# Attention's row sums and turned outputs on VectorE and by transfers within SBUF, beside the products with the values

## The chip, the cores and the metric

The kernel runs on one core of a Trainium2 chip. The metric is the device time of one execution in microseconds (us); before the change it is 2896.16 us, the median of three runs (2895.83 to 2897.63). Engines: TensorE (PE, and PEld for its weight loads), VectorE (DVE), ScalarE (ACT), GpSimd (POOL) and SyncE (SP), which here only issues transfers.

## What is computed

32 batches of a 512 x 512 matrix go through two graph layers that share one adjacency matrix. The first is attention with 8 heads of 64, masked by the adjacency matrix, then a residual and a layer norm without weights; the second multiplies by the adjacency matrix and a weight, again with a residual and a layer norm. Everything is float32.

```python
q, k, v = ((x @ W + b).reshape(b, n, 8, 64) for ...)
scores = einsum('bihd,bjhd->bhij', q, k) / sqrt(64) + where(adj == 0, -1e9, 0)
out = einsum('bhij,bjhd->bihd', softmax(scores), v)
x = layernorm(x + out)                     # layer 0
x = layernorm(x + (adj @ x) @ weight + bias)   # layer 1
```

## The kernel before

All 32 batches are unrolled into one program without loops on the chip; the order of every engine's instructions is written out by hand (a manual schedule), and each engine executes its own in that order. A wait holds everything behind it on its engine. `b` is the batch, `g` one of its two groups of four heads, `hp` one of its four pairs of heads (two in a group), `j` or `c` one of four blocks of 128 rows.

Scores are kept transposed: keys in the partitions, queries along the row. `scores` makes a group's scores pair by pair and block by block: two products with 64 rows of the array each (L555) into two PSUM banks, VectorE adds the mask and writes the tile `e` (L557), ScalarE takes the exponential in place (L559). GpSimd adds the four blocks of a pair into `es` (L570, `add_exponentials`), 128 x 1024 for two heads. `attend` multiplies by the values (L579) into one bank, a head's output in 64 partitions, so that the output too is transposed, and ScalarE copies it to `attT` (L582).

A row sum of the softmax is the sum of `es` over the partitions. `add_up` takes it on TensorE, by a product with ones (L590) for each head into 32 partitions of one bank; ScalarE copies it to `total` and adds it up for a check of the range (L596). `invert` turns `total` with four transposes on TensorE (L603), and VectorE takes the reciprocal (L605). `residual` turns `attT` with four transposes on TensorE for each pair (L612); VectorE multiplies by the reciprocals (L615) and adds to the rows of `x` (L617). After the last pair of a batch it calls `statistics` (L421, L422) for the layer norm, four blocks, each over whole rows.

All PSUM tiles come from `bank`, eight banks in turn. The main loop goes over (b, g): the products with the values of the group's pairs, `add_up`, the scores of the next group, then other work (`units_of`) by `work_until`, with `invert` and `residual` at set shares of it. That other work is: in the first half of a batch the projections of q and k of the next batch (L359, seven block products by Strassen's scheme each, evicted by VectorE and ScalarE), in the second half the rest of v, the product with the adjacency matrix of the batch before (`aggregate`, L478) and its convolution with the weight (`convolve`, seven block products, also L359). `convolve` evicts with VectorE: L531 adds a bank to `x`, for blocks 6 and 7 L527 updates the tile `mix` from the bank and GpSimd adds `mix` to `x` (L529); blocks run in the order 1, 2, 5, 6, 7, 3, 4, and the additions of 3 and 4 go to rows that GpSimd has added to. `flips` turns the input of the batch after next: VectorE's 32 x 32 transposes (L343, `turn_squares`), and GpSimd's four sums for Strassen's factors (`sum_rows`, L349, L321 to L323). VectorE's transpose turns each 32 x 32 square in its place only; that is why the input of those batches is loaded in squares of 32 columns (`load_squares`, L246: 16 transfers of 512 pieces of 128 B), which puts the squares in the places where they belong. The same sums for the aggregated rows are at the end of `aggregate` (L321 to L323).

SP issues in one queue: `load_squares(b + 2)`, which waits for the tiles `xin`, then in `turn_over` the store of batch b - 2 (L462) and the load of `x` of batch b (L231) into the same tile, which waits for the store to land. After the last group there is a tail for the last two batches.

Of the kernel before, what the change touches and what calls it, by code (L numbers as in the profile page):

```python
# [32 lines left out]
FP = mybir.dt.float32  # L36
# [3 lines left out]
AF = mybir.ActivationFunctionType  # L40
# [5 lines left out]
P = 128  # L46
# [159 lines left out]
def fast_kernel(ctx: ExitStack, tc, verdict, x, adj, Wq, bq, Wk, bk, Wv, bv, W1, b1, out):  # L206
# [14 lines left out]
    def bank(*shape):  # L221

        return psum.tile([P, *shape], FP, name="bank", tag="bank", bufs=8)
# [47 lines left out]

    ident = consts.tile([P, P], FP, name="ident")
    make_identity(nc, ident)
    ones = consts.tile([P, P // GROUP], FP, name="ones")
    nc.gpsimd.memset(ones, 1.0)
    eps = consts.tile([P, 1], FP, name="eps")
    nc.gpsimd.memset(eps, EPS)

    sums = consts.tile([P, B * (H // GROUP)], FP, name="sums")
    inverses = consts.tile([P, NB, GROUP], FP, name="inverses")  # L280
    nc.gpsimd.memset(inverses, 0.0)


# [54 lines left out]
    def turn_squares(b, d):  # L338

        if d == 0:  # L340
            XT[b] = work.tile([P, 7, 2, half], FP, name="yT" if b == 1 else "xT", bufs=1)
        xt = XT[b]
        nc.vector.transpose(xt[:, d // 2:d // 2 + 3:2, d % 2, :],  # L343
                            IN[b, d].rearrange("p j f -> p (j f)").rearrange("p (a n) -> p a n", a=2))
# [51 lines left out]
    def flips(b):  # L396

        return [(turn_squares if b else x_transpose, b, c) for c in range(NB)] + [(sum_rows, b)] if b < B else []
# [140 lines left out]
        return [(convolve, b, i) for i in (1, 2, 5, 6, 7, 3, 4)] if b >= 0 else []  # L539


    E, ES, AT, TOTAL, INVERSE = {}, {}, {}, {}, {}
    PAIRS = GROUP // 2

    def scores(b, g):
# [26 lines left out]
    def attend(b, hp):  # L572
        po = bank(N)
        for j in range(NB):
            e = E.pop((b, hp, j))
            for s in range(2):
                h = 2 * (hp % 2) + s
                values = V[b][hp // 2][:, j, h * HD:(h + 1) * HD]
                nc.tensor.matmul(po[s * HD:(s + 1) * HD, :], values, e[:, s, :],  # L579
                                 start=(j == 0), stop=(j == NB - 1))  # L580
        AT[b, hp] = work.tile([P, N], FP, name="attT")
        nc.scalar.activation(AT[b, hp], po, AF.Copy)  # L582

    def add_up(b, g):

        width = P // GROUP
        pm = bank(N)
        for h in range(GROUP):
            es = ES[b, (g * GROUP + h) // 2][:, h % 2, :]
            nc.tensor.matmul(pm[h * width:(h + 1) * width, :], ones, es, start=True, stop=True,  # L590
                             tile_position=(0, h * width))
        for hp in range(g * PAIRS, (g + 1) * PAIRS):
            ES.pop((b, hp))
        total = TOTAL[b, g] = work.tile([P, N], FP, name="total", bufs=1)
        at = b * (H // GROUP) + g
        nc.scalar.activation(total, pm, AF.Copy, accum_out=sums[:, at:at + 1])  # L596

    def invert(b, g):

        total = TOTAL.pop((b, g))  # L600
        pt = bank(NB, GROUP, P // GROUP)
        for c in range(NB):
            nc.tensor.transpose(pt[:, c, :, :], total[:, c * P:(c + 1) * P], ident)  # L603
        inverse = INVERSE[b, g] = work.tile([P, NB, GROUP], FP, name="inverse")
        nc.vector.reciprocal(inverse, pt[:, :, :, 0])  # L605
        nc.gpsimd.tensor_add(inverses, inverses, inverse)

    def residual(b, hp):
        at = AT.pop((b, hp))
        pt = bank(NB, 2, HD)  # L610
        for c in range(NB):
            nc.tensor.transpose(pt[:, c, :, :], at[:, c * P:(c + 1) * P], ident)  # L612
        first = 2 * hp % GROUP
        inverse = INVERSE[b, 2 * hp // GROUP][:, :, first:first + 2]
        nc.vector.tensor_mul(pt, pt, inverse[:, :, :, None].to_broadcast([P, NB, 2, HD]))  # L615
        cols = X[b][:, :, hp * P:(hp + 1) * P]
        nc.vector.tensor_add(cols, pt.rearrange("p c s d -> p c (s d)"), cols)  # L617
        if hp == HP - 1 and b < B - 1:
            for c in range(NB):
                statistics(b, 0, c)  # L620


    def judge():
        seen = consts.tile([P, 3], FP, name="seen")
        nc.vector.tensor_reduce(seen[:, 0:1], sums, axis=AX.X, op=ALU.add)
        nc.vector.tensor_reduce(seen[:, 1:2], inverses, axis=AX.XY, op=ALU.add)
        nc.vector.tensor_reduce(seen[:, 2:3], inexact, axis=AX.X, op=ALU.add)
        well = consts.tile([P, 3], FP, name="well")
        nc.vector.tensor_scalar(well[:, 0:2], seen[:, 0:2], BOUND, None, op0=ALU.is_le)
        nc.vector.tensor_scalar(well[:, 2:3], seen[:, 2:3], 0.0, None, op0=ALU.is_equal)  # L630
        nc.vector.tensor_mul(well[:, 0:1], well[:, 0:1], well[:, 1:2])
        nc.vector.tensor_mul(well[:, 0:1], well[:, 0:1], well[:, 2:3])
        return well[:, 0:1]


    def run(units):
        for unit in units:
            unit[0](*unit[1:])
# [10 lines left out]
        run(first[9 + c:10 + c])  # L649
    run(first[13:16])  # L650
    later = scores(0, 0)
    run(first[16:18] + later + first[18:] + [(look_for_low_half, c) for c in range(NB)] + flips(1))

    def norm(t, which):

        if t - which < 0:
            return []
        lo, hi = which * NB, (which + 1) * NB
        return [(square_root, t, slice(lo, hi)), (invert_root, t, slice(lo, hi))] + [
            (normalise, t, slot) for slot in range(lo, hi)]  # L660
# [5 lines left out]
    def weighed(units):  # L666

        weight = {project: 0.5, aggregate: 0.55, x_transpose: 0.13, convolve: 0.5}
        return [(u, weight.get(u[0], 0.0)) for u in units]

    def units_of(b):

        made, turned = projections(b + 1), flips(b + 2)
        splits, gathered = aggregation(b - 1)
        young, old, seen = norm(b - 1, 0) if b < B - 1 else [], norm(b - 1, 1), survey(b - 2)
        ready = [(turn_over, b)] if 1 < b < B - 1 else []
        if b == B - 1:


            older = convolution(b - 2)  # L680
            lows = [(split_low, b - 1, d) for d in range(DB - 1)]
            units = weighed(lows[:2] + older[:3] + lows[2:] + splits[3:] + older[3:] + gathered + seen)
            return units, [sum(w for _, w in units)] * 2

        if old:
            both = [[(f, b - 1, slice(0, 2 * NB))] for f in (square_root, invert_root)]
            behind = [seen[:2], seen[2:]] + both + [old[2:4], old[4:] + ready] + [[u] for u in young[2:]]
        else:
            behind = [ready] + [[u] for u in young]
        if b == 0:  # L690
            behind = [[]] + [[(sum_weights, w1, n)] for n in range(4)]
        behind += [[] for _ in range(11 - len(behind))] + [splits[:1], [], splits[1:2]]
        units = []
        for k, unit in enumerate(made[:16]):
            units += [unit] + (behind[k] if k < len(behind) else [])
        first = sum(w for _, w in weighed(units))
        values = made[16:]
        units += values[:3] + gathered[:1] + splits[2:3] + gathered[1:2] + values[3:] + splits[3:]
        if b == B - 2 > 0:
            units += [(load, B - 1)]  # L700
        units += gathered[2:3] + turned[:1] + gathered[3:]
        convolved = convolution(b - 1) if b < B - 2 else []
        for k in range(7):
            units += convolved[k:k + 1] + turned[k + 1:k + 2]
        units = weighed(units)
        return units, [first, sum(w for _, w in units)]

# [2 lines left out]
    for i, (b, g) in enumerate(groups):  # L710
# [19 lines left out]

        for hp in range(g * PAIRS, (g + 1) * PAIRS):
            attend(b, hp)
        add_up(b, g)
        if i == len(groups) - 1:
            break
        later = scores(*groups[i + 1])
        if g == 0 and b + 2 < B:
            load_squares(b + 2)
        work_until(0.35)
        invert(b, g)  # L740
        work_until((0.6 if b != B - 2 else 1.0) if g else 0.85)
        for hp in range(g * PAIRS, (g + 1) * PAIRS):
            residual(b, hp)
# [5 lines left out]
        release()  # L749
    t = B - 1  # L750
    rest, last = convolution(t - 1), convolution(t)
    run(rest[:1])
    invert(t, GROUPS - 1)
    for hp in range(HP - PAIRS, HP):
        residual(t, hp)
    old, seen = norm(t - 1, 1), survey(t - 1)
    run(old[:1] + rest[1:2] + old[1:])
    if t > 1:
# [14 lines left out]


    halves = {}

    def half_statistics(c, s):
        if c not in halves:
            halves[c] = work.tile([P, 2, nc.vector.BN_STATS_DIM], FP, name="halves", bufs=NB)
        nc.vector.bn_stats(halves[c][:, s, :], X[t][:, c, s * half:(s + 1) * half])  # L780

    old = norm(t, 1)
# [50 lines left out]
```

## Time and profile before

| | value |
|---|---|
| median of three runs | 2896.16 us |
| the profiled execution, its time | 2896.59 us |
| its span, first to last instruction | 2894.7 us |
| mean granted TensorE clock | 0.998 |
| scores: evictions L557, 1024 of them | 679 ns each |
| exponentials L559, 512 | 1053 ns each |
| sums of exponentials L570, 384 | 2425 and 2470 ns each, by form |
| row transfers L246, 496 | 64 KB each, 2.4 us from issue to landing |

The page of a profile gives each engine's busy time and share of the span, and then the chain of work that ended last, followed back from the last instruction through what released each step: what stands there set the time. A group's line names the source line, the engine, the operation, output <- inputs, the shape, the count; then the busy time in us, the mean of one in ns, and the idle time of the engine ahead of it with what ended it. TensorE executes a float32 product in two instructions, so its counts are twice the products (its transposes count once). In a timeline, the first two columns are start and length in us, and a last bracket gives the idle time before the instruction and what ended it.

### The profile page before, as it was taken

How to read it: one execution, taken by the hardware profiler on the slowest of the kernel's cores; microseconds unless marked ns; L12 is line 12 of the kernel's file. 1: busy time of each engine (PE TensorE's matmuls, PEld its weight loads, DVE VectorE, ACT ScalarE, POOL GpSimd, SP SyncE). 2: the span in 40 equal slices, each digit the busy share in tenths (PEclk: the TensorE clock that was granted, in tenths of full speed). 3: DMA queues.
4: the chain of work that ended last, by engine and by line, in shares of the span. 5: the costliest groups of instructions: out<-in, count | busy, mean ns of one | idle time of the engine just before them, and what ended most of it. 6: DMA issues, size and time to landing. Idle time of an engine off the chain costs nothing.

```text
span 2894.7 us, 36142 instructions
## 1 busy us (share of the span) xinstructions
PE 2866.6 (99%) x13602; PEld 1989.3 (69%) x13602; DVE 1775.3 (61%) x3095; ACT 1190.0 (41%) x1678; POOL 1743.8 (60%) x1092
## 2 busy tenths in 40 slices
PE   9999999999999999999999999999999999999997
PEld 6676776766767767667676676676766766767665
DVE  6655566656665666656656665566556665665675
ACT  3344353343433443434435344343344343443443
POOL 4665665565756657656566556575665766656654
PEclk9999999999999999999999999999999999999999
DMA  5101111111101111011111111110101101111001
GB/s 144 23 6 41 44 31 28 41 33 44 44 15 45 32 42 45 15 44 33 41 44 30 30 40 34 44 44 15 44 31 43 44 15 44 33 41 44 15 30 45
DMA packets 302579, 108.84 MB, mean 38 GB/s; under 512 B 264256, under 2 KB 268352, under 8 KB 302400
## 3 DMA queue, kind: packets, MB, share of 16 engines
q1 hardware_dynamic: 302400, 106.47, 14.4%
q8 instruction: 110, 1.80, 0.3%
q14 instruction: 69, 0.57, 0.1%
HBM read 72.88 MB, written 33.55 MB: 37 GB/s over the span
## 4 chain that ended last, share of the span: by engine, by line
PE 95%; DVE 2%; POOL 1%; ACT 1%; DMA 0%; issue 0%; SPq 0%; DVEq 0%; POOLq 0%; ACTq 0%
PE bank L359 52%; PE bank L555 15%; PE bank L579 15%; PE bank L478 8%; PE bank L590 2%; PE bank L612 2%; PE bank L603 1%; POOL es L570 1%; DVE e L557 0%; DVE bnst L421 0%; DMA xin<-in_x_dram 0%; DMA wq<-in_L_gnn_Wq_dram 0%; DVE attT L300 0%; POOL xs L452 0%; PE bank L505 0%
## 5 line engine op out<-in xcount | busy, mean ns | idle before, releaser
L557 DVE SCALAR_TENSOR_TENSOR e<-gap,bank 128x512 f32<-128x512 uint8 x1024 | 617.8, 679 | 284.4 <-PE bank L555 284.4
L570 POOL TENSOR_TENSOR es<-e 128x1024 f32<-128x1024 f32 x128 | 316.2, 2470 | 596.5 <-ACT e L559 596.5
L570 POOL TENSOR_TENSOR es<-es,e 128x1024 f32<-128x1024 f32 x256 | 620.7, 2425 | 20.1
L559 ACT ACTIVATE e<-e 128x1024 f32<-128x1024 f32 x512 | 524.1, 1053 | 102.3 <-DVE e L557 63.7
L582 ACT ACTIVATE attT<-bank 128x512 f32<-128x512 f32 x128 | 76.3, 597 | 1047.8 <-PE bank L579 1044.1
L555 PE MATMUL bank<-q,k 64*128 64x512 f32 x2048 | 464.2, 598 | 0.6 <-DVE e L557 0.6
L579 PE MATMUL bank<-e,v 128*64 128x512 f32 x2048 | 453.9, 595 | 1.9 <-DVE v L394 1.9
L359 PE MATMUL bank<-wv,xT 128*128 128x256 f32 x1736 | 398.0, 381 | 0.0
L359 PE MATMUL bank<-w,yT 128*128 128x256 f32 x1792 | 392.9, 379 | 1.6 <-DVE yT L510 1.6
L359 PE MATMUL bank<-xT,wk 128*128 128x256 f32 x1736 | 390.5, 379 | 0.7 <-DVE wk L309 0.7
L359 PE MATMUL bank<-xT,wq 128*128 128x256 f32 x1736 | 389.6, 382 | 1.4 <-DVE wq L309 1.1
L555 PEld LDWEIGHTS bank<-q,k 64*128 64x128 f32 x2048 | 204.3, 186 | 260.6 <-issue 196.8
L359 PEld LDWEIGHTS bank<-xT,wq 128*128 128x128 f32 x1736 | 328.2, 191 | 68.4 <-DVE e L557 22.7
L359 PEld LDWEIGHTS bank<-w,yT 128*128 128x128 f32 x1792 | 337.9, 190 | 48.0 <-DVE yT L510 2.0
L359 PEld LDWEIGHTS bank<-wv,xT 128*128 128x128 f32 x1736 | 322.7, 190 | 63.6 <-DVE e L557 23.5
L359 PEld LDWEIGHTS bank<-xT,wk 128*128 128x128 f32 x1736 | 327.3, 190 | 44.1 <-PE bank L359 1.1
L579 PEld LDWEIGHTS bank<-e,v 128*64 128x64 f32 x2048 | 141.7, 137 | 279.1 <-issue 268.2
L531 DVE TENSOR_TENSOR xs<-bank,xs 128x512 f32<-128x512 f32 x186 | 121.9, 669 | 187.3 <-POOL xs L529 182.3
L452 POOL TENSOR_TENSOR xs<-xs,b_r 128x512 f32<-128x512 f32 x124 | 157.8, 1274 | 114.5 <-DVE low L451 114.5
L529 POOL TENSOR_TENSOR xs<-xs,mix 128x512 f32<-128x512 f32 x93 | 117.3, 1275 | 175.0 <-DVE mix L527 175.0
L436 ACT ACTIVATE xs<-xs,shift,rstd 128x512 f32<-128x512 f32 x248 | 184.8, 810 | 27.3 <-DVE shift L431 27.3
L481 ACT ACTIVATE yT<-bank 128x512 f32<-128x512 f32 x124 | 74.1, 598 | 293.4 <-PE bank L478 293.4
(121 smaller groups left out, 2869.1 us busy)
## 6 DMA issues: line engine op xcount, KB each, us to landing
xin<-in_x_dram SPq DMA_DIRECT2D x496, 64.0 KB, 2.4
xs<-in_x_dram SPq DMA_DIRECT2D x31, 1024.0 KB, 5.2
out_dram<-xs SPq DMA_DIRECT2D x31, 1024.0 KB, 4.3
xin<-in_x_dram SPq DMA_DIRECT2D x4, 256.0 KB, 3.8
wq<-in_L_gnn_Wq_dram SPq DMA_DIRECT2D x2, 512.0 KB, 6.4
wk<-in_L_gnn_Wk_dram SPq DMA_DIRECT2D x2, 512.0 KB, 8.2
yT<-in_adj_dram SPq DMA_DIRECT2D x1, 1024.0 KB, 8.5
wv<-in_L_gnn_Wv_dram SPq DMA_DIRECT2D x2, 512.0 KB, 9.4
```

The lines of the kernel that those rows point to most:

```text
L359: nc.tensor.matmul(pm[:, r, :], left[:, d, r * P:(r + 1) * P], right[:, d, :], start=(d == 0), stop=(d == 1))
L436: nc.scalar.activation(row, row, AF.Identity, bias=SHIFT[t][:, slot:slot + 1], scale=RSTD[t][:, slot:slot + 1])
L452: nc.gpsimd.tensor_add(cols, cols, b1_r[:, None, d * P:(d + 1) * P].to_broadcast([P, NB, P]))
L478: nc.tensor.matmul(pm.rearrange("p a n -> p (a n)"), part, adjT[:, n % NB, :], start=(n == 0), stop=(n == 2 * NB - 1))
L529: nc.gpsimd.tensor_add(block, block, MIX[b])
L531: nc.vector.tensor_add(block, pm, block)
L555: nc.tensor.matmul(ps[s], keys[:, j * P:(j + 1) * P], queries, start=True, stop=True)
L557: nc.vector.scalar_tensor_tensor(e[:, s, :], gap[:, j, :], NEG * root, ps[s], op0=ALU.mult, op1=ALU.add)
L559: nc.scalar.activation(e, e, AF.Exp, scale=1.0 / root)
L570: nc.gpsimd.tensor_add(ES[b, hp], ES[b, hp] if j > 1 else E[b, hp, 0], E[b, hp, j])
L579: nc.tensor.matmul(po[s * HD:(s + 1) * HD, :], values, e[:, s, :], start=(j == 0), stop=(j == NB - 1))
L582: nc.scalar.activation(AT[b, hp], po, AF.Copy)
```

## The change

Row sums. `add_up`'s ones product, `total` and `invert` go. `fold_squares`, after the products of each pair, has VectorE turn the 32 x 32 squares of `es` (128 x 1024, into a tile from `e`'s eight buffers) and add up each square's rows (a reduction to 32 numbers per partition, tile `part`). `add_up`, now after the next group's scores, multiplies by `fold`, a matrix that adds the four squares of a column over the partitions: four products of 16 columns, one for each of 32 partitions of the output, which are then in the order that `residual` wants. VectorE takes the reciprocal, and adds the sums up for the check of the range.

Outputs. `turn_out` has VectorE turn the squares of a pair's output straight from PSUM (this takes ScalarE's copy away), and 16 transfers within SBUF put the squares in their places in the tile `rows`: 32 partitions x 4 x 32 numbers each, pieces of 128 B. In `residual` ScalarE multiplies `rows` by the reciprocals, 8 instructions of 128 x 64 for a pair, and GpSimd adds them to `x`. The last group of the last batch keeps TensorE's transposes.

Order. `flips(1)` and `look_for_low_half` at the start are moved; `sum_rows` in the second half goes from behind the fourth convolution block to behind the fifth (block 7 in the order above); `units_of`'s lists are adapted.

```diff
     def turn_squares(b, d):
...
-            XT[b] = work.tile([P, 7, 2, half], FP, name="yT" if b == 1 else "xT", bufs=1)
+            XT[b] = work.tile([P, 7, 2, half], FP, name="xT", bufs=1)
...
-        AT[b, hp] = work.tile([P, N], FP, name="attT")
-        nc.scalar.activation(AT[b, hp], po, AF.Copy)
+        SQUARES[b, hp] = work.tile([P, 2, N], FP, name="e", bufs=8)
+        OUT[b, hp] = po
+
+    def turn_out(b, hp):
+
+        po = OUT.pop((b, hp))
+        at = AT[b, hp] = work.tile([P, N], FP, name="attT")
+        if (b, hp // PAIRS) == (B - 1, HP // PAIRS - 1):
+            nc.scalar.activation(at, po, AF.Copy)
+            return
+
+        nc.vector.transpose(at, po)
+        turned = at.rearrange("p (c j f) -> p c j f", c=NB, j=P // SQ)
+        rows = ROWS[b, hp] = work.tile([P, NB, P], FP, name="rows")
+        for i in range(P // SQ):
+            for j in range(P // SQ):
+                nc.sync.dma_start(rows[j * SQ:(j + 1) * SQ, :, i * SQ:(i + 1) * SQ],
+                                  turned[i * SQ:(i + 1) * SQ, :, j, :])
+
+    def fold_squares(b, hp):
+
+        if hp % PAIRS == 0:
+            PART[b, hp // PAIRS] = work.tile([P, GROUP, N // SQ], FP, name="part", bufs=1)
+        square = SQUARES.pop((b, hp))
+        nc.vector.transpose(square.rearrange("p s n -> p (s n)"), ES.pop((b, hp)).rearrange("p s n -> p (s n)"))
+        heads = slice(2 * (hp % PAIRS), 2 * (hp % PAIRS) + 2)
+        nc.vector.tensor_reduce(PART[b, hp // PAIRS][:, heads, :], square.rearrange("p s (j f) -> p s j f", f=SQ),
+                                axis=AX.X, op=ALU.add)
 
     def add_up(b, g):
...
-            nc.tensor.matmul(pm[h * width:(h + 1) * width, :], ones, es, start=True, stop=True,
-                             tile_position=(0, h * width))
...
-        nc.scalar.activation(total, pm, AF.Copy, accum_out=sums[:, at:at + 1])
-
-    def invert(b, g):
...
-            nc.tensor.transpose(pt[:, c, :, :], total[:, c * P:(c + 1) * P], ident)
+        part = PART.pop((b, g)).rearrange("p h (j i) -> p i j h", i=P // SQ)
+        pm = bank(NB, GROUP)
+        for i in range(P // SQ):
+            nc.tensor.matmul(pm[i * SQ:(i + 1) * SQ, :, :], fold, part[:, i, :, :], start=True, stop=True,
+                             tile_position=(0, i * SQ))
         inverse = INVERSE[b, g] = work.tile([P, NB, GROUP], FP, name="inverse")
-        nc.vector.reciprocal(inverse, pt[:, :, :, 0])
+        nc.vector.reciprocal(inverse, pm)
+        nc.vector.tensor_add(sums, pm, sums)
         nc.gpsimd.tensor_add(inverses, inverses, inverse)
 
     def residual(b, hp):
         at = AT.pop((b, hp))
-        pt = bank(NB, 2, HD)
-        for c in range(NB):
-            nc.tensor.transpose(pt[:, c, :, :], at[:, c * P:(c + 1) * P], ident)
         first = 2 * hp % GROUP
         inverse = INVERSE[b, 2 * hp // GROUP][:, :, first:first + 2]
-        nc.vector.tensor_mul(pt, pt, inverse[:, :, :, None].to_broadcast([P, NB, 2, HD]))
         cols = X[b][:, :, hp * P:(hp + 1) * P]
-        nc.vector.tensor_add(cols, pt.rearrange("p c s d -> p c (s d)"), cols)
+        if (b, hp) in ROWS:
+            rows = ROWS.pop((b, hp))
+            for c in range(NB):
+                for s in range(2):
+                    part = rows[:, c, s * HD:(s + 1) * HD]
+                    nc.scalar.activation(part, part, AF.Identity, bias=zero, scale=inverse[:, c, s:s + 1])
+            nc.gpsimd.tensor_add(cols, cols, rows)
...
-            units += convolved[k:k + 1] + turned[k + 1:k + 2]
+            units += convolved[k:k + 1] + (turned[k + 1:k + 2] if k < 3 else turned[4:] if k == 4 else [])
...
         for hp in range(g * PAIRS, (g + 1) * PAIRS):
             attend(b, hp)
-        add_up(b, g)
+            fold_squares(b, hp)
+            turn_out(b, hp)
+            if i == 0 and hp == 0:
+                run(flips(1))
         if i == len(groups) - 1:
+            add_up(b, g)
             break
         later = scores(*groups[i + 1])
+        add_up(b, g)
         if g == 0 and b + 2 < B:
             load_squares(b + 2)
-        work_until(0.35)
-        invert(b, g)
         work_until((0.6 if b != B - 2 else 1.0) if g else 0.85)
```

## What is predicted, and how

> **What bounds the kernel now.** First the page: busy shares and the chain that ended last.
>
> ```profile
> PE 2866.6 (99%) x13602; PEld 1989.3 (69%) x13602; DVE 1775.3 (61%) x3095; ACT 1190.0 (41%) x1678; POOL 1743.8 (60%) x1092
> ...
> PE 95%; DVE 2%; POOL 1%; ACT 1%; DMA 0%; issue 0%; SPq 0%; DVEq 0%; POOLq 0%; ACTq 0%
> PE bank L359 52%; PE bank L555 15%; PE bank L579 15%; PE bank L478 8%; PE bank L590 2%; PE bank L612 2%; PE bank L603 1%; POOL es L570 1%; DVE e L557 0%; DVE bnst L421 0%; DMA xin<-in_x_dram 0%; DMA wq<-in_L_gnn_Wq_dram 0%; DVE attT L300 0%; POOL xs L452 0%; PE bank L505 0%
> ```
>
> TensorE is the bound, and L590, L612 and L603, which the change removes, are on the chain. But it is so only because the other engines are just in time, and 61% is a mean. So I read one steady batch: the chain from 1424 to 1514 us, then the timelines of VectorE and GpSimd there. From the chain:
>
> ```profile
> 1424.49 7.02 PE bank L579 x32
> 1431.51 1.00 PE bank L590 x8
> ...
> 1448.76 0.44 PE bank L603 x4
> ...
> 1456.38 0.87 PE bank L612 x8
> ...
> 1469.34 7.02 PE bank L579 x32
> ...
> 1513.63 0.57 PE bank L579
> ```
>
> A batch takes 1513.63 - 1424.49 = 89.14 us of unbroken TensorE work. Call A the start of the products with values of a batch's second group (1424.49), A' that of the next batch's first group (1469.34, A+44.85). The removed pieces cost 1.00 + 0.44 + 0.87 = 2.31 us a group. From the timelines of VectorE and GpSimd:
>
> ```profile
> 1460.17 0.69 DVE L421 BATCH_NORM_STATS2 bnst<-xs 128x6 f32<-128x512 f32 x1
> ...
> 1477.10 0.69 DVE L531 TENSOR_TENSOR xs<-bank,xs 128x512 f32<-128x512 f32 x1 [6.22 <-POOL xs L529]
> 1478.44 9.65 DVE L557 SCALAR_TENSOR_TENSOR e<-gap,bank 128x512 f32<-128x512 uint8 x16 [0.66 <-PE bank L555]
> ```
> ```profile
> 1438.33 2.37 POOL L570 TENSOR_TENSOR es<-e 128x1024 f32<-128x1024 f32 x1 [13.51 <-ACT e L559]
> ...
> 1461.36 1.26 POOL L323 TENSOR_TENSOR yT<-yT 128x512 f32<-128x512 f32 x1
> ```
>
> At A' VectorE has its last addition of the convolution over at 1477.79, 0.66 us before the first score bank (L557) wants it: the slack of this boundary. At the other boundary (A) it idles 8.3 us before L557. GpSimd runs without a break from 1438.33 to 1462.62.
>
> **What the Trainium skill says.** "VectorE: DVE Perf Modes", section "The perf-mode tier table (the rule you actually need)": `tensor_reduce` has one speed, an element per cycle. The trace agrees: 686 ns for 512 elements, as for other operations here. "SBUF — State Buffer", section "Who interferes with whom": VectorE work with one SBUF input doesn't contend with GpSimd, with two it does. The trace agrees: L343 stays within 667 to 704 ns, while L451, two SBUF inputs, takes 0.68 to 1.66 us. So transposes and reductions keep their price. "TensorE: Matmul & The Clock Gate", section "Part 1: The HAM clock gate (the "warmup" mystery)": an idle window of about 3.4 us halves the clock. The trace agrees: after 4.42 us without a matmul up to 2833.97, the granted clock of the next window is 0.66.
>
> **The change part by part**, all in times after A.
>
> TensorE. Removed 2.31 us a group. Added: `add_up`'s four products by `fold`, 16 columns each, each of two passes as all f32 products here. No row shows such; by L590 (1.00 us at 512 columns, four column tiles side by side) it is below that and above its weight load (0.16 us): I take 0.4, range 0.2 to 0.9. Net gain 1.9 us a group.
>
> VectorE, new before each group's scores: per head pair a 128x1024 transpose and a 128x1024 reduction, then a 128x512 transpose from PSUM. L343 takes 696 ns and L301 686 ns for 512 elements; at 1.04 ns for each further element 1024 take 1.22 us. With their dependence 1.25 + 1.15 + 0.62 = 3.0 us a pair, 6.0 a group. Removed are L615 and L617, 4 x 0.69 a group. Total 1775 + 64 x (6.0 + 0.3 for `sums`) - 126 x 1.38 = about 2000 us: no bound by sum.
>
> Boundary A. VectorE is free at A+0.8 and TensorE's products end at A+7.0; the first pair's work takes it to 3.3, its turn waits for the products to A+4.4, the second pair ends at A+7.8. The first eviction, 1.09 us after the scores' start (1433.59 - 1432.50), is wanted at A+8.1. Hidden; the cover is 0.3 us.
>
> Then the second-group residual moves from VectorE to ScalarE and GpSimd:
> - GpSimd's row begins 4.74 us after the first eviction (1438.33 - 1433.59), so at A+12.85, and lasts 24.3 us: A+37.15. The two residual additions stand behind it in its order, 2 x 1.25 us (L452's size): A+39.65.
> - ScalarE's 16 scalings of 128x64: L436 with the same two pointer operands shows 810 ns for 512, L384 469 for 256. "ScalarE: Activation LUTs", "What ACT_TABLE_LOAD costs" gives 186 ns + 93 for each pointer + 0.833 per element, less 93 of overlap: an estimate of 0.33 us each, 5.4 in all (0.25 to 0.41 by L436 and L425). From A+31.4 to A+36.8: beside GpSimd.
> - Rows. Transfers of 128 B runs within SBUF are not in the trace; L246's are alike in packets: 16 issues in 8.29 us, 0.52 each, landing after 2.4. The 32 of a group, from A+4.4, are in at about A+24, needed at A+31.4. Both bounds of the issue (0.31; 0.92 in the run's first loads) matter below only.
> - The statistics (L421) wait for GpSimd's second addition and stand in VectorE's queue ahead of the convolution's evictions. Before, they began at A+35.7 by VectorE's own work; now at A+39.65. They take 3.2 us (1460.17 to 1463.38): A+42.9. The evictions and transposes up to `mix` take 4.83 (to 1468.21): A+47.7.
> - Then the exchange over `mix`: GpSimd 1.27, VectorE 0.70, GpSimd 2.5, VectorE's last addition 0.67, with hand-overs 5.35: A+53.1. Moving `sum_rows` behind takes its 5 us out of this, which is why it isn't longer.
> - Now 6.0 us of the new vector work: A+59.1.
>
> TensorE meanwhile: A' = 44.85 - 2.31 + 0.4 = A+42.95, products to A+49.97; first eviction wanted at A+51.05. It comes 8.05 us late. Of eight banks two hold outputs that VectorE has not turned, so three of eight score pairs go ahead, then TensorE waits. The last pair is done 6.05 us after the first eviction, as in the trace (1478.44 to 1484.49). So a batch gains 3.8 us and loses 8.05: +4.2 us. VectorE is on time again in the first half, where it had waits of 4.8 us.
>
> That holds for the 29 boundaries (b = 1 to 29) where a convolution stands in the second half: +122 us. The other three batches gain 6 x 1.9 = 11 us, and lose at their own boundaries and in the tail, where L615 and L617 are on the chain (2.8 us, against 5.4 + 2.5 now): 0 to 40, taken as 18. Boundary waits of about 5 us can halve the clock; the scores are then paced by VectorE, so 0 to 1 us a boundary, taken as 0.2: 6.
>
> SP. In a batch it issues 64 row transfers, 16 of L246, then the store and the load of x (L462, L231), in one queue. From A+56, at 0.52: rows to A+73, L246 to A+81, the load lands at about A+95 after its wait for the store. GpSimd's residual of the first group wants it at A+89 and isn't needed for the next `es` until A+106: hidden.
>
> Sum: 2894.7 + 122 + 7 + 6 = 3029.7 of span, 1.9 more around it (the profiled execution: 2896.59); the median is 0.4 below that: 3031, rounded 3030 us.
>
> **The rivals.** A measurement here can tell 0.2%, 5.8 us, from no change.
> - Faster: VectorE's lateness at A' hides. Place: the scores' first eviction; the point from which it decides: a wait below 3.8 us a batch. The sum then is TensorE's alone: 2896 - 64 x 1.9 = 2775. For it: 99% TensorE, VectorE at 70%, boundary A. Against: at A' there were 0.66 us of slack, and 6.0 us come in behind a chain that itself grows.
> - Break-even: `mix` and the last addition end with the products (A+50); then only about 4.4 us wait and the time is about 2905.
> - Slower still: issues at 0.92. The load of x lands at A+110, GpSimd is 8 us late for `es`, and this passes down the chain above: 29 x 8 more, 3260. Decides from about 0.76 per issue. For it: 14.71 us for 16 at the start; against: those stood behind weight loads.
> - The change doesn't do what it says: the program's order shows the three matmul groups gone, so no.
>
> **How the numbers follow.** Forecast 0.78, its own range 2930 to 3130 (the chain 2.5 us shorter or longer, clock and tail at their ends); faster 0.12; break-even 0.05; slow issues 0.05. The range 2905 to 3140 leaves out about 0.18. Slower 0.84 (forecast, slow issues, part of break-even), same 0.04, faster 0.12.
>
> **What would show it.** Right: in the chain, VectorE, GpSimd and ScalarE hold some 10 to 15%; scores waiting for VectorE, 7 to 9 us, 29 times, the reduction or the turn right before L557; statistics that wait for GpSimd; TensorE busy below 95%. Wrong: statistics that begin before A+37; new vector work below 5 us a group; a scaling well off 0.33 us doesn't matter below 0.5. Row transfers that ScalarE waits for would show the last rival; TensorE back at 99% the first.

## The result, and the profile after

The changed kernel takes 3044.09 us, the median of four runs (3042.89 to 3044.3), against 2896.89 us (four runs) of the kernel before on the same chip: ratio 1.0508, 95% interval 1.0489 to 1.0526. It is 147 us slower; 3030 was forecast. Its profiled span is 3041.4 us, the mean granted clock 0.962 (0.998 before).

From the profile's page of the changed kernel: TensorE's busy share, then the chain of what ended last, by engine and by line. Up to the scores' exponentials, lines of the old program have numbers some ten higher (L555 is now L565, L557 L567, L421 L431, L531 L541).

```profile
PE 2893.8 (95%) x12842; PEld 1995.6 (66%) x12842; DVE 2016.7 (66%) x3289; ACT 1403.4 (46%) x2432; POOL 1900.4 (62%) x1223
...
PE 46%; POOL 28%; DVE 15%; issue 6%; ACT 3%; DVEq 0%; SPq 0%; POOLq 0%; DMA 0%; ACTq 0%
PE bank L369 30%; POOL es L580 14%; PE bank L565 8%; PE bank L589 8%; POOL xs L539 4%; DVE bnst L431 3%; POOL xs L462 3%; POOL xs L643 3%; DVE xs L541 2%; DVE e L615 2%; ACT e L569 2%; DVE e L567 2%; DVE attT L602 1%; POOL v L401 1%; DVE xT L353 1%
```

The three groups that TensorE lost are gone (13602 instructions before, 12842 now), yet TensorE holds only 46% of the chain, 95% before. TensorE's busy time has even risen, since products released one by one or at a lower clock take longer: the scores L565 617.2 us, 468.6 in the fastest version below, in which they hardly wait (6.9 us in all). GpSimd and VectorE took its place on the chain, and their lines are those of one stretch: sums of exponentials, bias, residual, statistics, exchange, new vector work.

One boundary, in VectorE's timeline of the changed kernel. Columns: start, busy time, line, operation, tiles; in brackets the idle time before it and what ended it. The batch's second group starts its products with values at A = 1496.31.

```profile
1528.01 0.42 DVE L493 TENSOR_TENSOR yT<-bank,yT 128x256 f32<-128x256 f32 x1 [1.14 <-ACT yT L491]
1535.95 0.69 DVE L431 BATCH_NORM_STATS2 bnst<-xs 128x6 f32<-128x512 f32 x1 [7.52 <-POOL xs L643]
...
1539.16 0.66 DVE L541 TENSOR_TENSOR xs<-bank,xs 128x512 f32<-128x512 f32 x1
...
1543.34 0.65 DVE L537 TENSOR_TENSOR mix<-bank,mix 128x512 f32<-128x512 f32 x1
...
1548.67 0.69 DVE L541 TENSOR_TENSOR xs<-bank,xs 128x512 f32<-128x512 f32 x1 [2.00 <-POOL xs L539]
1549.28 1.24 DVE L615 STREAM_TRANSPOSE e<-es 128x1024 f32<-128x1024 f32 x1
1550.55 1.22 DVE L617 TENSOR_REDUCE part<-e 128x32 f32<-128x1024 f32 x1
1551.68 0.71 DVE L602 STREAM_TRANSPOSE attT<-bank 128x512 f32<-128x512 f32 x1
...
1554.69 0.71 DVE L602 STREAM_TRANSPOSE attT<-bank 128x512 f32<-128x512 f32 x1
1555.32 9.62 DVE L567 SCALAR_TENSOR_TENSOR e<-gap,bank 128x512 f32<-128x512 uint8 x16
```

VectorE stands idle 7.52 us until GpSimd's residual addition L643, and from there its queue runs on to the first eviction L567, with two short waits for GpSimd in the exchange over `mix`. The same boundary in TensorE's timeline:

```profile
1546.37 2.84 PE L565 MATMUL bank<-q,k 64*128 64x512 f32 x10
1549.42 1.12 PE L565 MATMUL bank<-q,k 64*128 64x512 f32 x2 [0.20 <-DVE xs L541]
1552.44 2.07 PE L565 MATMUL bank<-q,k 64*128 64x512 f32 x2 [1.91 <-DVE attT L602]
1555.45 6.21 PE L565 MATMUL bank<-q,k 64*128 64x512 f32 x18 [0.93 <-DVE attT L602]
1561.59 0.26 PE L625 MATMUL bank<-part,fold 128*32 128x16 f32 x8
```

Ten of the 32 score instructions (five products, one bank each) go ahead, then TensorE waits for a bank three times: once for VectorE's last addition of the exchange, twice for its turn of an output. The stretch from the first product to the last takes 15.3 us here instead of 7.2.

The starts of the groups of products with values give the balance. From the second group of batch 1 to that of batch 30, 29 batches, a batch takes 93.90 us where it took 89.15: +138 us. The stretch ahead of it is 4.2 us longer, the stretch behind it 4.5 us. Together 147.

### The profile page after: what moved, and what is told of

Same layout as the page of the kernel before. It is cut to its first block, busy times and chain, and to the rows that moved or that the text cites. A ratio compares the mean times of both kernels' runs of the same rounds, so it can differ in the third digit from the quotient of the medians.

```text
span 3041.4 us, 39256 instructions
## 1 busy us (share of the span) xinstructions
PE 2893.8 (95%) x12842; PEld 1995.6 (66%) x12842; DVE 2016.7 (66%) x3289; ACT 1403.4 (46%) x2432; POOL 1900.4 (62%) x1223
## 4 chain that ended last, share of the span: by engine, by line
PE 46%; POOL 28%; DVE 15%; issue 6%; ACT 3%; DVEq 0%; SPq 0%; POOLq 0%; DMA 0%; ACTq 0%
PE bank L369 30%; POOL es L580 14%; PE bank L565 8%; PE bank L589 8%; POOL xs L539 4%; DVE bnst L431 3%; POOL xs L462 3%; POOL xs L643 3%; DVE xs L541 2%; DVE e L615 2%; ACT e L569 2%; DVE e L567 2%; DVE attT L602 1%; POOL v L401 1%; DVE xT L353 1%
## 5 line engine op out<-in xcount | busy, mean ns | idle before, releaser
L565 PE MATMUL bank<-q,k 64*128 64x512 f32 x2048 | 617.2, 678 | 109.2 <-DVE attT L602 102.5
L567 DVE SCALAR_TENSOR_TENSOR e<-gap,bank 128x512 f32<-128x512 uint8 x1024 | 616.7, 676 | 10.8 <-PE bank L565 10.8
L565 PEld LDWEIGHTS bank<-q,k 64*128 64x128 f32 x2048 | 289.7, 212 | 435.1 <-DVE attT L602 164.1
L369 PE MATMUL bank<-xT,wk 128*128 128x256 f32 x1792 | 403.0, 379 | 0.7 <-DVE wk L319 0.7
L369 PE MATMUL bank<-xT,wq 128*128 128x256 f32 x1792 | 402.5, 382 | 1.2 <-DMA wq<-in_L_gnn_Wq_dram 0.9
L369 PEld LDWEIGHTS bank<-xT,wk 128*128 128x128 f32 x1792 | 340.2, 190 | 47.2 <-PE bank L369 1.1
L369 PEld LDWEIGHTS bank<-xT,wq 128*128 128x128 f32 x1792 | 338.8, 191 | 48.3 <-ACT xT L344 1.2
L369 PEld LDWEIGHTS bank<-wv,xT 128*128 128x128 f32 x1792 | 337.5, 190 | 47.5 <-DVE e L567 0.8
L642 ACT ACTIVATE rows<-rows,zero,inverse 128x64 f32<-128x64 f32 x1008 | 340.6, 426 | 4.6 <-DMA rows<-attT 4.2
L431 DVE BATCH_NORM_STATS2 bnst<-xs 128x6 f32<-128x512 f32 x248 | 165.6, 668 | 237.7 <-POOL xs L643 237.7
L643 POOL TENSOR_TENSOR xs<-xs,rows 128x512 f32<-128x512 f32 x124 | 156.0, 1280 | 159.0 <-DMA xs<-in_x_dram 159.0
```

Source lines behind the costliest of these rows:

```text
L369: nc.tensor.matmul(pm[:, r, :], left[:, d, r * P:(r + 1) * P], right[:, d, :], start=(d == 0), stop=(d == 1))
L431: nc.vector.bn_stats(st, X[b][:, c, :])
L565: nc.tensor.matmul(ps[s], keys[:, j * P:(j + 1) * P], queries, start=True, stop=True)
L567: nc.vector.scalar_tensor_tensor(e[:, s, :], gap[:, j, :], NEG * root, ps[s], op0=ALU.mult, op1=ALU.add)
L642: nc.scalar.activation(part, part, AF.Identity, bias=zero, scale=inverse[:, c, s:s + 1])
L643: nc.gpsimd.tensor_add(cols, cols, rows)
```

## The experiments

All times are medians against runs of the kernel before on the same chip (2895.9 to 2897.2 us). Each edit is to the changed kernel unless said otherwise; where it adds a line, lines below stand one higher (L615 is then L616).

### The statistics out of the way (stats_late)

The statistics of a batch's last residual are collected and emitted behind the next group's scores, so that VectorE's queue no longer waits for GpSimd ahead of the exchange.

```diff
         if hp == HP - 1 and b < B - 1:
-            for c in range(NB):
-                statistics(b, 0, c)
+            seen_later.extend((statistics, b, 0, c) for c in range(NB))
+            if b == B - 2:
+                run(seen_later)
+                seen_later.clear()
...
         later = scores(*groups[i + 1])
         add_up(b, g)
+        run(seen_later)
+        seen_later.clear()
```

> The changed kernel with one thing moved: the four statistics after a batch's last residual come behind the scores of the next group on VectorE instead of ahead of the convolution's evictions (the batch before the last keeps their place). Same instructions, same counts. Theory 'waiting statistics': 237.7 us of VectorE's idle time before L431 end with GpSimd's residual addition, and everything up to the scores' evictions stands behind. Without them VectorE follows TensorE through the convolution, the exchange over mix ends at about A+45, the new vector work at A+51.1, just when the first score eviction is wanted (A+51.05): no wait, clock back near 1.0, 29 x (89.14 - 4.24) for the steady batches, some +8 in start and tail: 2785 us (2770 to 2805). Rival 'the 6 us of vector work at the boundary are the price': at least 4.4 us of wait remain, about 2905.

Measured: 2849.18 us (2847.74 to 2850.03), ratio 0.9838 (0.9822 to 0.9855), the clock back at 0.996. So 195 us of the changed kernel hang on the place of these eight instructions a batch. But 64 us of the gain expected are missing: the scores take 9.6 us, 2.4 more than they need. VectorE's timeline in this run:

```profile
1425.92 0.42 DVE L493 TENSOR_TENSOR yT<-bank,yT 128x256 f32<-128x256 f32 x1 [1.13 <-ACT yT L491]
1431.69 0.69 DVE L541 TENSOR_TENSOR xs<-bank,xs 128x512 f32<-128x512 f32 x1 [5.35 <-ACT mix L535]
```

and ScalarE's:

```profile
1425.78 5.40 ACT L643 ACTIVATE rows<-rows,zero,inverse 128x64 f32<-128x64 f32 x16
1431.08 0.58 ACT L535 ACTIVATE mix<-bank 128x512 f32<-128x512 f32 x1
```

The wait for GpSimd is gone and another stands behind it: the exchange's first addition waits for ScalarE's copy of the same bank to `mix`, and that copy is queued behind the 16 new scalings.

### The copy ahead of the scalings as well (best)

```diff
-        work_until((0.6 if b != B - 2 else 1.0) if g else 0.85)
+        work_until((0.62 if b != B - 2 else 1.0) if g else 0.85)
```

> Edit on top of the run with the late statistics: the residual of a batch's second group is emitted after the first block of the second projection (0.6 becomes 0.62 in the planner), so ScalarE copies that block out (the mix copy) before its 16 scalings, not after them. Theory (ScalarE's queue is the second link): in the run with the late statistics VectorE's chain began 5.35 us late on that copy; now it can begin as soon as TensorE has the block, some 4.6 us earlier; GpSimd's residual adds then hold the exchange, which gets 2.4 us earlier. The stretch of scores was 9.6 us there for 7.2 of products, so these 2.4 us per batch go: 2849 - 29 x 2.4 = 2779 us (2765 to 2800), faster than both kernels. Rival (the 2.4 us are the vector work itself, or GpSimd): 2849 again.

Measured: 2779.54 us (2779.07 to 2780.31), ratio 0.9597 (0.9581 to 0.9613): 117 us below the kernel before and 265 below the change as it was. A batch takes 85.22 us, 3.93 less than before. Its page:

```profile
PE 2743.4 (99%) x12842; PEld 1913.0 (69%) x12842; DVE 2017.7 (73%) x3289; ACT 1403.0 (51%) x2432; POOL 1911.1 (69%) x1223
...
PE 96%; POOL 2%; DVE 1%; issue 0%; ACT 0%; DMA 0%; SPq 0%; POOLq 0%; DVEq 0%; ACTq 0%
```

and its boundary in VectorE's timeline, with the next products with values starting at A' = 1404.38:

```profile
1394.76 0.69 DVE L541 TENSOR_TENSOR xs<-bank,xs 128x512 f32<-128x512 f32 x1 [1.30 <-ACT mix L535]
...
1405.92 0.69 DVE L541 TENSOR_TENSOR xs<-bank,xs 128x512 f32<-128x512 f32 x1 [2.02 <-POOL xs L539]
1406.53 1.23 DVE L616 STREAM_TRANSPOSE e<-es 128x1024 f32<-128x1024 f32 x1
...
1412.57 1.87 DVE L568 SCALAR_TENSOR_TENSOR e<-gap,bank 128x512 f32<-128x512 uint8 x3
```

The first eviction starts 8.19 us after A'; by the prediction it is wanted 7.02 + 1.09 = 8.11 us after. All the new work is in, VectorE has the same work (2017.7 us busy, 2016.7 in the changed kernel), and TensorE holds 96% of the chain again. The wait is only just gone: this schedule has no slack there.

### The copy ahead of the scalings, alone (mix_first)

The edit of the run before, with the statistics left in place.

> The move of the residual behind the first block alone, with the statistics in their place. Theory (two links in series, the later one decides): the statistics still wait for GpSimd's residual adds, which end as late as before or up to 1.7 us later since the scalings now stand behind the copy; only the first addition of the exchange, 0.6 us, is ahead of them. Nothing is gained: 3044 + 29 x (-0.7 to +1.7) = 3025 to 3095 us, 3045 taken. Rival (the copy behind the scalings was the whole delay and the late statistics helped only by the way): the 4.6 us per batch go here too, about 2905.

Measured: 3021.22 us (3020.81 to 3021.7), ratio 1.0431 (1.0414 to 1.0449). 23 us less than the change, 0.8 a batch, just below the range expected. The statistics begin 40.0 us after A (39.6 before), held by GpSimd as before; but not only the first addition, also one transpose of x passes ahead of them, 1.2 us in place of the 0.6 assumed. The rival's 2905 is far off. The two waits stand in series: moving the later one alone brings 195 us, the earlier one alone 23, both together 265.

### The order of the exchange put back (old_order)

```diff
-            units += convolved[k:k + 1] + (turned[k + 1:k + 2] if k < 3 else turned[4:] if k == 4 else [])
+            units += convolved[k:k + 1] + turned[k + 1:k + 2]
```

> The changed kernel with the place of sum_rows undone: GpSimd's four sums for the input (L359, L331 to L333) stand again between the additions of block 6 and of block 7 of the convolution. Theory 'one chain through GpSimd': they are 5.04 us (1469.52 to 1474.56 in the trace before) and lie in the exchange over mix, which now sets the start of the scores' evictions: 29 x 5.0 more, 3190 us (3175 to 3220, the clock may drop longer). Rival 'GpSimd has 38% to spare and orders of its own don't count': 3044, no change.

Measured: 3190.75 us (two runs, 3188.97 and 3192.53), ratio 1.1018 (1.0996 to 1.104). Two lines of this run's waits (what was waited for, us in total, times, longest):

```profile
DVE bnst L431 <- POOL xs L643: 237.7, 31, 11.2
DVE xs L541 <- POOL xs L539: 180.9, 30, 6.2
```

The first is as in the changed kernel (237.7); the second was 60.1 there. `sum_rows` between GpSimd's two additions of the exchange puts its four additions into the chain, but for the 0.8 us that GpSimd idled there anyway: the first eviction comes 4.2 us later (A+63.2 for A+59.0). The other 0.8 of the 5.0 us a batch stand behind the first eviction, where the granted clock is halved for longer (13.7 us a boundary, 6.8 in the changed kernel). That the 5.0 of the expectation is met is in part luck: it counted the additions alone at their full length. The change's own reordering was worth 147 us at this boundary.

### The scalings left out (no_scale)

Of the 8 scalings of a pair only the first is executed; the other seven eighths of `rows` go undivided into the residual.

```diff
             for c in range(NB):
                 for s in range(2):
                     part = rows[:, c, s * HD:(s + 1) * HD]
-                    nc.scalar.activation(part, part, AF.Identity, bias=zero, scale=inverse[:, c, s:s + 1])
+                    if c == 0 and s == 0:
+                        nc.scalar.activation(part, part, AF.Identity, bias=zero, scale=inverse[:, c, s:s + 1])
```

> The changed kernel with one of eight scalings by ScalarE for a pair kept and seven left out (7/8 of the division by the row sums are left out). Theory: ScalarE's 16 scalings end at A+36.9 in the trace after, GpSimd's sums of exponentials and combinations at A+37.1; GpSimd is the later, so nothing changes: 3044 us (3038 to 3050). Rival 'the 1008 small instructions of ScalarE are on the path': up to 4.7 us a batch less, down to 2905.

Measured: 3043.74 us (two runs, 3043.58 and 3043.91). ScalarE lost 289 us of work (1403.4 to 1114.1) and the kernel none: in the change as it stands GpSimd's additions come later than the scalings. The scalings count only where the statistics have been taken away, as the first run showed, and there by what is queued behind them.

### The sums made early (fold_early)

The first group's sums are made in place ahead of the last residual of the batch before, in the stretch in which VectorE waits for GpSimd.

```diff
+        if g and b < B - 2:
+            for hp in range(PAIRS):
+                fold_squares(b + 1, hp, early=True)
         for hp in range(g * PAIRS, (g + 1) * PAIRS):
             residual(b, hp)
```

> The sums of a batch's first group (both transposes, done in place, and both reductions) are emitted ahead of the last residual of the batch before it, where VectorE stood idle 7.5 us for GpSimd's residual adds; statistics and residuals stay where the change put them. Theory (what is behind the exchange on VectorE is added to the wait one to one): 2 x (1.22 + 1.22) = 4.9 us per batch less in front of the first eviction, the halved clock after the wait goes too (0.4): 3044 - 29 x 5.1 = 2896 us (2875 to 2915). Rival (the wait for GpSimd sets the time and the vector work hides in it): 3044.

Measured: 2879.41 us (2877.63 to 2880.16), ratio 0.994 (0.9923 to 0.9956). In VectorE's timeline of this run the sums lie inside the wait, which shrinks from 7.52 to 2.77 us:

```profile
1448.20 1.23 DVE L616 STREAM_TRANSPOSE es<-es 128x1024 f32<-128x1024 f32 x1
...
1451.88 1.22 DVE L618 TENSOR_REDUCE part<-es 128x32 f32<-128x1024 f32 x1
1455.87 0.70 DVE L431 BATCH_NORM_STATS2 bnst<-xs 128x6 f32<-128x512 f32 x1 [2.77 <-POOL xs L644]
```

A batch gains 5.7 us: 5.1 at those boundaries where the clock cost little (15.3 us of scores there, 10.2 here), more at the others. The vector work behind the exchange was part of the wait one to one (the first eviction is 4.8 us earlier, A+54.25 for A+59.03); what is more than that goes with the granted clock, which stays at full speed at these boundaries. The same instructions cost nothing in a gap of the same engine.

### The sums alone, and what was left in them (sums_only, sums_fold, sums_late)

Outputs are turned by TensorE as before the change (ScalarE copies them, VectorE divides and adds); the sums are VectorE's. In `turn_out` and in the main loop:

```diff
-        if (b, hp // PAIRS) == (B - 1, HP // PAIRS - 1):
+        if True:
             nc.scalar.activation(at, po, AF.Copy)
             return
...
-            fold_squares(b, hp)
             turn_out(b, hp)
+            fold_squares(b, hp)
```

> The row sums alone by VectorE (squares of es turned, reduced, folded); the outputs as before the change: copied by ScalarE, turned by TensorE, multiplied and added by VectorE, so that statistics don't wait for GpSimd. Theory 'one shared chain': VectorE's residual ends at A+34.4, statistics at A+37.6, evictions at A+42.4, mix exchange at A+47.8, 4.8 us of squares and reductions to A+52.6; wanted at A+50.5: 2.1 us of wait against 2 x 1.25 us of TensorE work gained: 2890 us (2870 to 2910). Rival 'VectorE's added work costs by its length': the sums are 4.8 of the 6.0 us, so most of the +147: about 3010.

Measured: 2859.27 us (2857.62 to 2860.05), ratio 0.9872 (0.9855 to 0.9888), 31 us below what was expected. Without the residual on GpSimd the statistics start 34.8 us after A (1440.08 - 1405.3), and the scores lose 0.85 us a batch (8.06 us for 7.21; 0.83 in the expectations below) where I had counted on 2.1. Two attempts at this rest, first with the early sums of the run before:

> The run with the sums alone, with the first group's sums made early as in the run with the early sums; outputs are turned by TensorE. Theory (the 0.83 us that scores still lost at each of the 29 boundaries there are vector work behind the exchange): they go, 2859 - 29 x 0.83 = 2835 us (2828 to 2850); the full change with late statistics and the early copy, 2779.5, is then worth 55 us more than its first half at its best. Rival (the early sums push the residual and so the exchange back by as much as they take out behind it): 2859 or more.

Measured: 2872.21 us (2871.0 to 2873.38), ratio 0.9914 (0.9898 to 0.9931). The rival held. In this order VectorE has no gap there: a batch takes 87.81 us as without it (87.80), and at the start of the program 12 us are lost. Then with the statistics behind the scores:

> The run with the sums alone, with the statistics of a batch's last residual behind the next scores as in the run with the late statistics; outputs are turned by TensorE. Theory (the early sums failed since in that order VectorE had no idle time ahead of the residual, so 4.9 us in front of the exchange made it 4.9 us later; the 0.83 us left per boundary are still what VectorE does between the residual and the first eviction): the statistics are 3.3 us of that stretch, so the 0.83 us go: 2859 - 29 x 0.83 = 2835 us (2825 to 2848). Rival (the exchange has some other floor, TensorE's blocks or GpSimd): 2859.

Measured: 2831.56 us (2831.25 to 2832.52), ratio 0.9776 (0.976 to 0.9792); the scores take 7.21 us, nothing is lost. So with the waits gone the sums bring 66 us, and turning the outputs 52 more (2831.6 to 2779.5). The outputs' half alone was not tried, so the 52 us are its worth on top of the sums only.

## Why the prediction was right

**The side and the mechanism.** 3030 was forecast, 3044.09 measured. The rivals' times were 2775 (the wait hides), 2905 (the exchange ends with the products) and 3260 (slow issues). The first is the time of another order: 2779.5 is what the same work takes when the wait is gone, which agrees with the sum of TensorE's part (2775). That 14 us are missing at the end and no more is in part luck: two terms were off in opposite directions, as shown below.

**TensorE.** `fold`'s products were taken at 0.4 us a group; they are 0.26 in the timeline (0.19 on the chain). The gain, taken as 1.9 a group, is 1.81 in one half of a batch (44.85 to 43.04) and, with the wait gone, 2.11 in the other (44.29 to 42.18 in the best version): 3.93 a batch, 3.8 forecast. At boundary A the cover of 0.3 us is there: VectorE waits 0.33 us for the first score bank (10.8 us in 33 waits).

**The chain after A**, forecast and then measured at the boundary shown: GpSimd's last residual addition over A+39.65, statistics from A+39.64; `mix` A+47.7 and A+47.7 (1543.99); the exchange over A+53.1 and A+53.0; the first eviction A+59.1 and A+59.0. The transposes and reductions, 1.22 us each by an extrapolation, have means of 1221 and 1220 ns. The scaling is 0.34 us in a row of 16, 0.33 forecast, with a mean of 426 ns since neighbours overlap. This agrees with the price of the Trainium skill, "ScalarE: Activation LUTs", "What ACT_TABLE_LOAD costs": 186 + 2 x 93 + 64 x 0.833 = 425 ns without overlap.

**What was late, and by how much.** 8.05 us were forecast. The first eviction comes at A'+15.99 on average, and at A'+8.18 where nothing waits (the run sums_late): 7.8 us late. The whole stretch of scores grew from 7.21 to 15.90 on average, by 8.7; the rest is the clock's, below. One detail was different: I had two of eight banks held, and a third was held too, by the exchange's last addition. It changed nothing, as the evictions set the pace.

**The term that was mis-sized: the clock.** Taken as 0.2 us a boundary, 6 in all. The last score product ends 6.05 us after the first eviction in the kernel before, and 6.93 after it on average in the changed one: 0.88 us a boundary, 25.5 in all. The boundaries alternate, with 15.3 us of scores at one (6.3 of it behind the first eviction) and 16.4 at the next (7.5). Stretches of 2 us of two boundaries that follow each other, in the changed kernel; columns: stretch, its length, busy us and instructions of PE, PEld, DVE, ACT and POOL, the granted clock, DMA share, GB/s:

```profile
1552.00:1554.00 2.00, 1.55 (x2) 0.50 (x2) 1.97 (x3) 0.00 (x0) 1.65 (x2) 0.50 0.05 8
1556.00:1558.00 2.00, 2.00 (x6) 1.32 (x6) 2.00 (x4) 1.20 (x2) 0.00 (x0) 0.50 0.16 25
1558.00:1560.00 2.00, 2.00 (x10) 1.52 (x8) 2.00 (x4) 1.86 (x2) 1.01 (x1) 0.80 0.16 25
...
1648.00:1650.00 2.00, 1.25 (x3) 1.09 (x5) 2.00 (x5) 0.05 (x1) 0.00 (x0) 0.50 0.16 25
1652.00:1654.00 2.00, 2.00 (x7) 1.48 (x5) 2.00 (x5) 1.72 (x3) 1.72 (x1) 0.50 0.16 25
1654.00:1656.00 2.00, 2.00 (x8) 0.88 (x5) 2.00 (x5) 1.72 (x3) 1.92 (x2) 0.90 0.16 25
```

Both have 6.8 us at half the clock. At the first they began at 1552, while TensorE waited anyway, and 3.5 us of them lie behind the first eviction (1555.32); VectorE's evictions nearly set the pace of the last 18 instructions (6.21 us). At the second they began near 1648, just ahead of these instructions, which took 7.34 us; 5.8 us lie behind the first eviction (1648.61). In the runs fold_early and stats_late, where the clock stays up at these boundaries, the scores end 6.01 us after the first eviction. So the 29 batches lost 29 x (7.81 - 3.93) = 112.5 us by the wait, less TensorE's gain, where the sum had 122, and 25.5 by the clock, where it had 6: 138. The other three batches and the tail took 4.2 + 4.5 = 8.7 us, 7 forecast.

Why the drop falls early at one boundary and late at the next can be read from the trace's record of the granted clock. In the changed kernel, in mix_first and in old_order the clock changes only on a grid of 3.413 us: the half-clock stretches are one to four of these steps long. A batch of the changed kernel is 93.90 us, 27.5 steps, so the grid lies half a step further on at each boundary, and every second boundary is alike. In mix_first (93.13 us, 27.3 steps) the stretch of scores runs through three or four lengths, from 16.1 down to 14.4 us, and begins again; in old_order (98.90 us, 29.0 steps) all boundaries but the first few have the same 21.0 us. What such a drop costs thus depends on the length of a batch, and one boundary doesn't tell it.

**The signs.** Most came as named: the scores wait 7.8 us at 29 boundaries, with a turn right before L567, and the statistics wait for GpSimd. Two did not: TensorE is busy 95% and not less, and VectorE, GpSimd and ScalarE hold 46% of the chain, where 10 to 15% were forecast. The forecast counted the wait alone; but the chain that ended last passes through these engines all the way from the evictions behind A to those behind A' (1504.50 to 1555.45 in one batch), and TensorE works beside it:

```profile
1503.39 1.11 PE bank L565 x4
1504.50 1.28 DVE e L567 x2
...
1533.47 2.46 POOL xs L643 x2
1535.95 0.71 DVE bnst L431
...
1554.69 0.72 DVE attT L602
1555.45 6.21 PE bank L565 x18
```

Two readings in the prediction were off and changed nothing: L451 takes up to 2.85 us in the kernel before, not 1.66; and the break-even rival's 4.4 us don't follow from its words, as 6.0 us of work from A+50 on are 4.9 us late and, with the forecast's other terms, give about 2935 us, inside the forecast's own range.

**SP and the row transfers.** They were forecast harmless and are: the rows land after 1.8 us, issued some 0.6 us apart (an issue takes 599 ns in the median, 0.52 taken); the load of x is issued at A+90.6 and lands after 5.1, A+95.7 (A+95 forecast). GpSimd waited for it 159 us in 28 places, and its next sums had time.

## What to carry to other kernels

Before moving work from the engine that is full to those that are not, follow one batch's dependent chain through the receiving engines' queues up to the instruction that the full engine waits for: here 117 us of gain were hidden under 265 us of waiting, and no busy share of the kernel before showed it. A wait added to an in-order queue counts by what is queued behind it; so ask first which instructions behind it are wanted soon and which are not (statistics, a division, a sum), and let the latter wait behind the former. Waits in series show one after the other: taking away the last one brings the next into view, and the steps have to be read again.

## What was not expected of the hardware

- A stretch in which TensorE has its products released one at a time by VectorE, with gaps of about 2 us (none of 4 us), is enough to halve the granted clock for 6.8 us: at the two boundaries shown TensorE was busy for 1.8 and 1.1 of the 3.4 us ahead of the drop. It cost 0.3 or 1.4 us, by how much of the half-clock stretch lay behind the first eviction.
- The granted clock changes on a grid of 3.413 us. With a batch of 27.5 steps the cost alternates from batch to batch; with 29.0 steps (old_order) it is the same in each.
- Four small f32 products with 16 columns (eight instructions), on four column tiles, take 0.26 us for all.
- A transpose of 32 x 32 squares straight from PSUM takes 712 ns for 128 x 512, hardly more than from SBUF (696 on average in the kernel before).
